# A stage woven by hand in steps of seven chunks, one norm product on ScalarE, and more convolution chunks on VectorE

## Chip, cores, metric

The kernel runs on one core of a Trainium2 chip. The metric is the device time of one execution in microseconds. A core has five engines, each with its own queue that runs in order: TensorE (PE, with its weight loads shown apart as PEld), VectorE (DVE), ScalarE (ACT), GpSimd (POOL) and SyncE (SP), which starts the DMAs. Semaphores join the queues.

## The reference, cut to what matters

Four layers run over x of shape (2, 56, 56, 128): two images, 3136 tokens each, 128 channels. The change lies in layer 1 (a selective scan over four groups of 32 channels, called heads), and in the way from it to layer 2's attention; one small reordering reaches layer 0.

```python
def _vss_block(x, p):
    return x + _ss2d(_layernorm(x, p['ln1_w'], p['ln1_b']), p)
...
# layer 1, with prev of one head going into the next
prev = _vss_block(chunks[0], p) + vss_skip * chunks[0]
outs = [prev]
for i in range(1, g):
    s = prev + chunks[i]
    prev = _vss_block(s, p) + vss_skip * s
    outs.append(prev)
x_res = cvm_skip * x_orig + jnp.concatenate(outs, axis=3)
x = _layernorm(x_res, final_ln_w, final_ln_b)
...
# inside _ss2d: project in, 3x3 depthwise convolution, silu, four scans, then
y = _layernorm(y, p['out_norm_w'], p['out_norm_b']) * jax.nn.silu(z)
return y @ p['out_proj_w'].T
...
# layer 2
t = _to_tokens(x)
t = t + _L2_attn_ref(_ln_t(t))      # queries, keys and values are all _ln_t(t)
```

## The kernel before

Tokens are tiled into 28 rows of 112 for each image; four rows make a chunk of 448 tokens, so there are seven chunks, numbered 0 to 6. X holds all tokens of both images by token (112 partitions x 28 x 2 x 128). In layer 1 both images go together: 64 inner channels of each fill the 128 partitions.

Layer 1 has four scan blocks, one a head. Between them lie short stages, run by `Layer1.run`. For head 1 to 3 its loop goes over steps c = 0 to 7: `after(head - 1, c)` finishes chunk c of the head before, `before(head, c)` prepares chunk c of the next. Ahead of head 0, layer 0's own loop calls `before` in the same manner. After the last head the loop calls `after`, `last` (the final norm) and `chunk` of attention 2 for each chunk: this is the stage between layer 1's last scan and attention 2 (the second of the four layers is layer 1, counted from zero). Steps that follow one another in a stage:

- `gated_tokens` (L486 to L507): pm, the mean over channels by a matmul (PE); yc = y - pm (VectorE, L490); its square (ScalarE, L492); yc times the gate (GpSimd, L494); then for each of four token tiles three products, pv, p1, p2 (PE, L504, "p" in the text: 24 matmul records); rs, a square root on ScalarE (L506) and its reciprocal on VectorE (L507).
- `after` (L861 to L866): t = p1 times rs, plus p2 (VectorE), plus the old token values (GpSimd, L863); s and xo, two multiply-adds into the head's own values and into X (VectorE, L864, L866).
- `layernorm_tokens` (L77 to L84): sum, mean, subtraction (VectorE), square (ScalarE), sum of squares (VectorE), root (ScalarE), reciprocal (VectorE), product (GpSimd, L84). It is used for a head's input (nrm), for the final norm (X, with statistics in stf), and for attention 2's input (U, with stu).
- `last` multiplies X by a weight and adds a bias, both on GpSimd (L876): X's three GpSimd products are L84 and twice L876.
- `Attention2.chunk`: U, the norm of X; for each image four transposes to channels (PE, L1102), an evacuation that goes in turn to VectorE and ScalarE (L64, L68), and the key tiles: transposes back (PE, L1242) and another evacuation.
- `before` (L822 to L846): the head's input, its norm, four transposes pt (PE, L830) and hT (ScalarE, L831), a projection (L833) written into pad (ScalarE, L834), a padded image; a second projection and a silu for the gate z (L845, L846). At step c it also convolves chunk c - 1, which needs one row of chunk c in pad.
- `conv_rows`: the convolution by nine PE matmuls with diagonal weights (L455), or by nine taps on VectorE (L459, L461); then silu (ScalarE, L462) and a copy in column order (GpSimd, L463). Even steps go to VectorE, odd ones to PE:

```python
"DVE" if c % 2 == 0 else "PE",
```

The order of the instructions outside the scans comes from the framework's scheduler, which may move an instruction ahead of others within its engine; inside a block marked `manual_schedule` (as the scans are) the program order stands. Pools give the buffers: `mid1` has two of each name, `pmid1` one of each PSUM name, `pa2` two PSUM banks. After the woven stage, `mixer_filters` (L1297 to L1309) builds filter tables before attention 2 begins its first scores (L1034); the mixer's small weight sums (L1345 to L1364, L1666) are scheduled into the stage by VectorE's order. The next scan begins with a spread matmul, b (L359), and a product, h (L412).

Of the kernel before, what the change touches and what calls it, by code (L numbers as in the profile page):

```python
# [21 lines left out]
B = 2  # L22
# [47 lines left out]

def layernorm_tokens(k, out, x, sq, st, d, by=None):


    nc = k.nc
    g = x.shape[1]
    mean, var = st[:, 0, :], st[:, 1, :] if by is None else by
    nc.vector.tensor_reduce(mean, x, AX.X, ALU.add)  # L77
    nc.vector.tensor_scalar_mul(mean, mean, 1.0 / d)
    nc.vector.tensor_tensor(out, x, mean.unsqueeze(2).to_broadcast([TP, g, d]), ALU.subtract)
    nc.scalar.activation(sq, out, AF.Square)  # L80
    nc.vector.tensor_reduce(var, sq, AX.X, ALU.add)
    nc.scalar.activation(var, var, AF.Sqrt, bias=k.eps[:TP], scale=1.0 / d)
    nc.vector.reciprocal(var, var)
    nc.gpsimd.tensor_tensor(out, out, var.unsqueeze(2).to_broadcast([TP, g, d]), ALU.mult)  # L84

# [389 lines left out]

def gated_tokens(k, pools, nch, y, gate, avg, mean, w1, w2, c, nb):

# [7 lines left out]
    for ci in range(nch):  # L485
        nc.tensor.matmul(pm, lhsT=avg, rhs=y[ci][:, cs], start=ci == 0, stop=ci == nch - 1)  # L486
    sq, yz = [], []
    for ci in range(nch):
        yc = sp.tile([128, CH], F32, name=f"yc{ci}")
        nc.vector.tensor_tensor(yc, y[ci][:, cs], pm, ALU.subtract)  # L490
        s = one.tile([128, CH], F32, name=f"sq{ci}")
        nc.scalar.activation(s, yc, AF.Square)  # L492
        sq.append(s)
        nc.gpsimd.tensor_tensor(yc, yc, gate[ci], ALU.mult)  # L494
        yz.append(yc)
    n = w1[0].shape[-1]
# [3 lines left out]
    for i in range(4):  # L500
        ts = slice(TP * i, TP * (i + 1))
        for out, m, rhs in ((pv[:, nb * i : nb * (i + 1)], sq, [mean] * nch), (p1[:, i], yz, w1), (p2[:, i], gate, w2)):
            for ci in range(nch):
                nc.tensor.matmul(out, lhsT=m[ci][:, ts], rhs=rhs[ci], start=ci == 0, stop=ci == nch - 1)  # L504
    rs = sp.tile([TP, 4 * nb], F32, name="rs")
    nc.scalar.activation(rs, pv, AF.Sqrt, bias=k.eps[:TP])  # L506
    nc.vector.reciprocal(rs, rs)  # L507
    return p1, p2, rs
# [45 lines left out]
def layer0(k, d, big, follow):  # L554
# [3 lines left out]
    with ExitStack() as ctx:  # L558
# [42 lines left out]
        with ExitStack() as sctx:  # L601
# [65 lines left out]
            def after(b, pools, c, outs, bias):  # L667
# [9 lines left out]
                for ci in range(2):  # L677
# [6 lines left out]
                    gate.append(z)  # L684
                p1, p2, rs = gated_tokens(k, pools, 2, y, gate, avg, avg[:, 0:1], outs[0], outs[1], c, 1)
                t = one.tile([TP, 4, C], F32, name="t")
# [40 lines left out]
class Layer1:  # L727
# [82 lines left out]
    def before(self, head, pools, c, pad):  # L810
# [27 lines left out]
        if c > 0:  # L838
            conv_rows(
                k, (sp, vp), pad, self.diag, W["taps"], W["conv_b"], self.row, self.col, c - 1,  # L840
                "DVE" if c % 2 == 0 else "PE",
            )
# [6 lines left out]

    def after(self, head, pools, c):  # L850
        k, nc, D, R = self.k, self.k.nc, self.D, self.R
        sp, pp = pools
        gate = [self.z[:, CH * c : CH * (c + 1)]]
        p1, p2, rs = gated_tokens(k, (sp, pp, sp), 1, [self.y], gate, self.avg, self.mean, *self.outs, c, B)
        t = sp.tile([TP, 4 * B, D], F32, name="t")
# [5 lines left out]
        nc.vector.tensor_tensor(t, tokens(p1), rs.unsqueeze(2).to_broadcast([TP, 4 * B, D]), ALU.mult)  # L861
        nc.vector.tensor_tensor(t, t, tokens(p2), ALU.add)
        nc.gpsimd.tensor_tensor(t, t, s, ALU.add)  # L863
        nc.vector.scalar_tensor_tensor(s, s, R["vss_skip"], t, ALU.mult, ALU.add)  # L864
        xo = self.chunk(self.channels(head), c)
        nc.vector.scalar_tensor_tensor(xo, xo, R["cvm_skip"], s, ALU.mult, ALU.add)  # L866

    def last(self, sp, c):

# [3 lines left out]
        st = sp.tile([TP, 2, 4 * B], F32, name="stf")  # L873
        layernorm_tokens(k, xv, xv, sq, st, C)
        for op, n in ((ALU.mult, "final_ln_w"), (ALU.add, "final_ln_b")):
# [17 lines left out]
    def run(self, follow):  # L893
# [3 lines left out]
        for head in range(1, 5):  # L897
            self.scans.run()
            with ExitStack() as ctx:
# [4 lines left out]
                else:  # L904
                    sp = ctx.enter_context(k.pool("mid1", 2))
                    chunk = follow(ctx)
                for c in range(NCH + 1):
                    if c < NCH:
                        self.after(head - 1, (sp, pp), c)
                    if head < 4:  # L910
                        self.before(head, (sp, pp, self.vp), c, pad)
                    elif c < NCH:
                        self.last(sp, c)
                        chunk(c)

# [160 lines left out]
class Attention2:  # L1076
# [9 lines left out]
    def start(self, ctx):  # L1086
        self.sp = ctx.enter_context(self.k.pool("a2u", 2))
        self.pp = ctx.enter_context(self.k.pool("pa2", 2, psum=True))
        return self.chunk

    def chunk(self, c):
# [5 lines left out]
        flat = "p j b c -> p (j b) c"  # L1097
        layernorm_tokens(k, U.rearrange(flat), k.X[:, 4 * c : 4 * (c + 1)].rearrange(flat), sq, st, C)
        for b in range(B):
            pt = bank(self.pp, "pt")[:, 0:CH]  # L1100
            for i in range(4):
                nc.tensor.transpose(pt[:, TP * i : TP * (i + 1)], U[:, i, b, :], k.ident[:TP, :TP])  # L1102
            k.evacuate(self.uT[b][:, CH * c : CH * (c + 1)], pt)
            key_tiles(k, bank(self.pp, "pt"), self.uT[b], self.V[b], c)

# [882 lines left out]
```

## Time and profile before

| what | value |
|---|---|
| runs of the kernel before | 9179.0 us median of 3 (9177.25 to 9184.39) |
| the profiled execution | 9196.55 us |
| its span in the trace | 9194.7 us |
| mean granted TensorE clock | 0.947 |
| GpSimd's product L425 in the scans | 3755.4 us, 2048 times, 1859 ns each |
| VectorE's scan L353 | 2788.5 and 900.7 us, 1536 and 512 times |
| convolution matmuls L455 | 468 in all, 538 ns median, 1115 at most |
| stage from the first way into head 0 | 2766 to 2904 us |
| the ways into heads 1, 2 and 3 | 3547 to 3657, 4292 to 4401, 5037 to 5152 us |
| stage from the last scan to attention 2 | 5795 to 5947 us |

A line of a timeline gives the start in us, the duration in us, the engine, the line of the kernel, the operation, and what it writes and reads by name; in square brackets how long the engine had been idle and what released it. A line of windows gives the busy time of each engine in that stretch. Busy shares of the whole span average over stages with different limits, so a stage is read from its own windows.

### The profile page before, as it was taken

The page shows a single profiled execution, that of the slowest core. Times are in us where ns is not written, and L with a number is a line of the kernel's source. Part 1 is how long each engine was busy: PE and PEld are TensorE (multiplying, and loading weights), DVE is VectorE, ACT ScalarE, POOL GpSimd, SP SyncE. Part 2 cuts the span into 40 slices and gives each one's busy share as a digit, 9 for nine tenths or more (in the row PEclk, how much of TensorE's full clock was granted, in tenths as well). Part 3 has the DMA queues.
Part 4 walks back from the last instruction along what each step waited for, and adds up shares of the span by engine and source line. Part 5 has one row for each costly group of instructions (what it writes and reads, how often), then busy time and mean ns, then how long its engine had stood idle before and what let it go on. Part 6 is the DMA issues. An engine that isn't in the chain of part 4 may idle for free.

```text
span 9194.7 us, 93730 instructions
## 1 busy us (share of the span) xinstructions
PE 8062.6 (88%) x28825; PEld 4797.1 (52%) x28825; DVE 7113.2 (77%) x7587; ACT 3845.9 (42%) x6551; POOL 6325.5 (69%) x4023
## 2 busy tenths in 40 slices
PE   7888888888888888888888888699999999999998
PEld 3444445444445444444444444355688888874555
DVE  8999998999996997998899799611466666665442
ACT  4555545555555555555554555234211111114331
POOL 5999996999995996997899699666311111115551
PEclk9999999999998998999999899699999999999998
DMA  5666664666663994986798599100233333320003
GB/s 155 222 220 220 222 214 129 220 220 220 221 220 102 229 225 120 223 227 157 190 227 208 136 228 227 49 3 3 71 104 101 109 93 106 95 62 7 14 5 129
DMA packets 781377, 1364.55 MB, mean 148 GB/s; under 512 B 133213, under 2 KB 406494, under 8 KB 780842
## 3 DMA queue, kind: packets, MB, share of 16 engines
q1 hardware_dynamic: 780874, 1358.56, 52.4%
q8 instruction: 228, 3.74, 0.2%
q14 instruction: 275, 2.25, 0.1%
HBM read 1318.63 MB, written 39.60 MB: 148 GB/s over the span
## 4 chain that ended last, share of the span: by engine, by line
PE 38%; DVE 11%; issue 5%; ACT 3%; POOL 2%; DMA 1%; SPq 0%; DVEq 0%; POOLq 0%; ACTq 0%
PE cv L1516 12%; PE av L1028 6%; PE sc L1034 5%; DVE h L353 5%; PE pj L1630 4%; DVE h L412 3%; PE acc L373 2%; DMA c<-rows 1%; ACT a L334 1%; PE b L161 1%; PE cv L1578 1%; PE pcv L455 1%; POOL p L425 1%; PE every L1796 1%; PE lo L969 1%
## 5 line engine op out<-in xcount | busy, mean ns | idle before, releaser
L425 POOL TENSOR_TENSOR p<-h,c 128x784 f32<-128x784 f32 x2048 | 3755.4, 1859 | 125.5 <-DVE h L353 38.6
L373 PE MATMUL acc<-p,ident 128*128 128x392 f32 x8192 | 2990.4, 499 | 23.0 <-POOL p L425 21.8
L353 DVE TENSOR_TENSOR_SCAN h<-a,state,h 128x784 f32<-128x784 f32 x1536 | 2788.5, 1837 | 48.7 <-ACT a L334 27.4
L373 PEld LDWEIGHTS acc<-p,ident 128*128 128x128 f32 x8192 | 1487.3, 193 | 1043.8 <-POOL p L425 80.4
L412 DVE TENSOR_TENSOR h<-du,b 128x784 f32<-128x784 f32 x1408 | 1332.7, 947 | 96.5 <-PE b L359 91.4
L334 ACT ACTIVATE a<-delta,L0A 128x784 f32<-128x784 f32 x1024 | 939.3, 918 | 968.5 <-DVE h L353 965.8
L334 ACT ACTIVATE a<-delta,L1A 128x784 f32<-128x784 f32 x1024 | 939.0, 917 | 918.9 <-DVE h L353 916.1
L359 PE MATMUL b<-three,sel 96*128 96x512 bf16 (+1 forms) x2816 | 730.9, 342 | 572.7 <-DVE h L412 475.6
L428 POOL TENSOR_TENSOR h<-du,b 128x784 f32<-128x784 f32 x640 | 1187.8, 1856 | 0.0
L1047 POOL TENSOR_TENSOR total<-total,e 128x448 f32<-128x448 f32 (+1 forms) x644 | 735.8, 1143 | 325.1 <-ACT e L1036 285.2
L359 PEld LDWEIGHTS <-sel 96*128 96x128 bf16 x2816 | 282.6, 100 | 1243.2 <-issue 1065.4
L353 DVE TENSOR_TENSOR_SCAN h<-a,h 128x784 f32<-128x784 f32 x512 | 900.7, 1777 | 33.7 <-ACT a L334 23.4
L1529 DVE TENSOR_TENSOR u<-u,cv 128x512 f32<-128x512 f32 x1024 | 623.4, 679 | 326.9 <-PE cv L1516 325.6
L1560 POOL TENSOR_TENSOR u<-u,S 128x1024 f32<-128x1024 f32 x64 | 150.1, 2367 | 1039.2 <-DVE S L1529 1039.2
L1036 ACT ACTIVATE e<-sc 128x448 f32<-128x448 f32 (+1 forms) x700 | 377.5, 543 | 722.8 <-PE sc L1034 594.8
L1531 ACT COPY u<-cv 128x512 f32<-128x512 f32 x256 | 149.4, 587 | 826.7 <-PE cv L1516 773.3
L1630 PE MATMUL pj<-u,Wm 128*128 128x196 f32 (+8 forms) x1536 | 351.5, 382 | 5.7 <-DVE A L1636 5.7
L1034 PE MATMUL sc<-big 128*128 128x448 f32 (+1 forms) x700 | 323.4, 548 | 12.3 <-ACT e L1036 12.3
L1028 PE MATMUL av<-e,big 128*128 128x448 f32 (+1 forms) x700 | 320.7, 545 | 1.2 <-DVE e L1041 1.1
L1610 POOL TENSOR_TENSOR both<-mpm 128x512 f32<-128x512 f32 x32 | 40.6, 1270 | 395.0 <-DVE Wm L1666 271.5
L1630 PEld LDWEIGHTS pj<-u,Wm 128*128 128x128 f32 x1536 | 266.6, 191 | 70.4 <-issue 45.7
L973 DVE TENSOR_REDUCE m<-lo 112x1 f32<-112x448 f32 x392 | 229.2, 617 | 95.4 <-PE lo L969 95.1
(438 smaller groups left out, 10866.9 us busy)
## 6 DMA issues: line engine op xcount, KB each, us to landing
c<-rows SPq DMA_DIRECT2D x1024, 392.0 KB, 4.0
c<-rows SPq DMA_DIRECT2D x2048, 196.0 KB, 4.8
b<-rows SPq DMA_DIRECT2D x320, 392.0 KB, 4.5
b<-rows SPq DMA_DIRECT2D x640, 196.0 KB, 4.6
H<-raw SPq DMA_DIRECT2D x32, 1568.0 KB, 7.6
wC<-win SPq DMA_DIRECT2D x64, 576.0 KB, 6.2
w<-in_L_weight_dram SPq DMA_DIRECT2D x52, 512.0 KB, 5.3
wA<-win SPq DMA_DIRECT2D x64, 384.0 KB, 5.5
```

What stands on the lines that cost most here:

```text
L334: self.k.nc.scalar.activation(x["a"], g["delta"][ci], AF.Exp, scale=self.w["A"](g["kd"], ci, x["n"]))
L353: self.k.nc.vector.tensor_tensor_scan(h, a, h, start, ALU.mult, ALU.add)
L359: self.k.nc.tensor.matmul(ps[:, c0:c1], lhsT=self.w["selB"](x["n"]), rhs=x["g"]["three"][:, c0:c1], start=True, stop=True)
L373: nc.tensor.matmul(job["acc"][:, i, 0:392], lhsT=self.k.ident, rhs=x["p"][:, 392 * i : 392 * (i + 1)], start=False, stop=n == NS - 1,)
L412: nc.vector.tensor_tensor(one["h"], one["g"]["du"][one["ci"]], one["b"], ALU.mult)
L425: nc.gpsimd.tensor_tensor(now["p"], now["h"], now["c"], ALU.mult)
L428: nc.gpsimd.tensor_tensor(three["h"], three["g"]["du"][three["ci"]], three["b"], ALU.mult)
L1028: nc.tensor.matmul(acc, lhsT=V[b][:n, j, :], rhs=e[:n], start=j == 0, stop=j == NKT - 1)
L1034: nc.tensor.matmul(ps[:n], lhsT=keys[b][:, KT * j : KT * j + n], rhs=q, start=True, stop=True)
L1047: nc.gpsimd.tensor_tensor(total[:n], total[:n], e[:n], ALU.add)
L1516: self.k.nc.tensor.matmul(ps[:, b], lhsT=v[:, C * b : C * (b + 1)], rhs=h, start=i == 0, stop=i == len(terms) - 1)
L1630: nc.tensor.matmul(ps[:, lo - c0 : hi - c0], lhsT=Ws[f][:, eo, r, :], rhs=u[:, b, f, lo - a0 : hi - a0], start=f == 0, stop=f == 1,)
```

## The change

Seven chunks of the stage after the last head run as generators, each cut into 22 steps by `yield`. `woven` starts a new chunk every five ticks and advances every active chunk by one step in each tick, the oldest first; the block is marked `manual_schedule`, so this order stands in every queue. In that stage U's last product, 112 x 1024 on GpSimd, becomes eight ScalarE copies with a scale, 112 x 128 each. The pool `pa2` gets four PSUM banks instead of two. In layer 0, which uses the same gated function, the two subtractions now come ahead of the two squares. In `before`, step 5's convolution goes to VectorE for heads 1 to 3, and steps 3 and 5 for head 0: nine matmuls less and nine taps more for each.

```diff
--- before.py
+++ after.py
@@ -68,7 +68,28 @@
             self.nc.scalar.copy(out, in_)
 
 
-def layernorm_tokens(k, out, x, sq, st, d, by=None):
+def all_of(steps):
+
+
+    while True:
+        try:
+            next(steps)
+        except StopIteration as e:
+            return e.value
+
+
+def woven(stages, apart):
+
+    stages, active, at = list(stages), [], 0
+    while stages or active:
+        if stages and at % apart == 0:
+            active.append(stages.pop(0))
+        active = [one for one in active if next(one, active) is not active]
+        at += 1
+
+
+def layernorm_steps(k, out, x, sq, st, d, by=None, last="POOL"):
+
 
 
     nc = k.nc
@@ -77,11 +98,24 @@
     nc.vector.tensor_reduce(mean, x, AX.X, ALU.add)
     nc.vector.tensor_scalar_mul(mean, mean, 1.0 / d)
     nc.vector.tensor_tensor(out, x, mean.unsqueeze(2).to_broadcast([TP, g, d]), ALU.subtract)
+    yield
     nc.scalar.activation(sq, out, AF.Square)
+    yield
     nc.vector.tensor_reduce(var, sq, AX.X, ALU.add)
+    yield
     nc.scalar.activation(var, var, AF.Sqrt, bias=k.eps[:TP], scale=1.0 / d)
+    yield
     nc.vector.reciprocal(var, var)
-    nc.gpsimd.tensor_tensor(out, out, var.unsqueeze(2).to_broadcast([TP, g, d]), ALU.mult)
+    if last == "POOL":
+        nc.gpsimd.tensor_tensor(out, out, var.unsqueeze(2).to_broadcast([TP, g, d]), ALU.mult)
+    else:
+        yield
+        for i in range(g):
+            nc.scalar.activation(out[:, i], out[:, i], AF.Copy, scale=var[:, i : i + 1])
+
+
+def layernorm_tokens(*args, **more):
+    all_of(layernorm_steps(*args, **more))
 
 
 def tokens_to_channels(k, pool, dst, src):
@@ -473,7 +507,7 @@
     nc.gpsimd.memset(pad[:, :, PAD - 1 : PAD], 0.0)
 
 
-def gated_tokens(k, pools, nch, y, gate, avg, mean, w1, w2, c, nb):
+def gated_steps(k, pools, nch, y, gate, avg, mean, w1, w2, c, nb):
 
 
 
@@ -485,14 +519,18 @@
     for ci in range(nch):
         nc.tensor.matmul(pm, lhsT=avg, rhs=y[ci][:, cs], start=ci == 0, stop=ci == nch - 1)
     sq, yz = [], []
+    yield
     for ci in range(nch):
         yc = sp.tile([128, CH], F32, name=f"yc{ci}")
         nc.vector.tensor_tensor(yc, y[ci][:, cs], pm, ALU.subtract)
+        yz.append(yc)
+    yield
+    for ci, yc in enumerate(yz):
         s = one.tile([128, CH], F32, name=f"sq{ci}")
         nc.scalar.activation(s, yc, AF.Square)
         sq.append(s)
         nc.gpsimd.tensor_tensor(yc, yc, gate[ci], ALU.mult)
-        yz.append(yc)
+    yield
     n = w1[0].shape[-1]
     pv = pp.tile([TP, 4 * nb], F32, name="pv")
     p1 = pp.tile([TP, 4, n], F32, name="p1")
@@ -502,8 +540,10 @@
         for out, m, rhs in ((pv[:, nb * i : nb * (i + 1)], sq, [mean] * nch), (p1[:, i], yz, w1), (p2[:, i], gate, w2)):
             for ci in range(nch):
                 nc.tensor.matmul(out, lhsT=m[ci][:, ts], rhs=rhs[ci], start=ci == 0, stop=ci == nch - 1)
+    yield
     rs = sp.tile([TP, 4 * nb], F32, name="rs")
     nc.scalar.activation(rs, pv, AF.Sqrt, bias=k.eps[:TP])
+    yield
     nc.vector.reciprocal(rs, rs)
     return p1, p2, rs
 
@@ -682,7 +722,7 @@
                     z = sp.tile([128, CH], F32, name=f"z{ci}")
                     nc.scalar.activation(z, ps, AF.Silu, bias=W["in_b"][:, 2 + ci : 3 + ci])
                     gate.append(z)
-                p1, p2, rs = gated_tokens(k, pools, 2, y, gate, avg, avg[:, 0:1], outs[0], outs[1], c, 1)
+                p1, p2, rs = all_of(gated_steps(k, pools, 2, y, gate, avg, avg[:, 0:1], outs[0], outs[1], c, 1))
                 t = one.tile([TP, 4, C], F32, name="t")
                 nc.vector.tensor_tensor(t, p1, rs.unsqueeze(2).to_broadcast([TP, 4, C]), ALU.mult)
                 nc.vector.tensor_tensor(xr, xr, p2, ALU.add)
@@ -838,7 +878,7 @@
         if c > 0:
             conv_rows(
                 k, (sp, vp), pad, self.diag, W["taps"], W["conv_b"], self.row, self.col, c - 1,
-                "DVE" if c % 2 == 0 else "PE",
+                "DVE" if c in ((2, 3, 4, 5, 6) if head == 0 else (2, 4, 5, 6)) else "PE",
             )
         if c < NCH:
             ps = vp.tile([128, CH], F32, name="pcv")
@@ -848,10 +888,13 @@
             self.scans.first(vp)
 
     def after(self, head, pools, c):
+        all_of(self.after_steps(head, pools, c))
+
+    def after_steps(self, head, pools, c):
         k, nc, D, R = self.k, self.k.nc, self.D, self.R
         sp, pp = pools
         gate = [self.z[:, CH * c : CH * (c + 1)]]
-        p1, p2, rs = gated_tokens(k, (sp, pp, sp), 1, [self.y], gate, self.avg, self.mean, *self.outs, c, B)
+        p1, p2, rs = yield from gated_steps(k, (sp, pp, sp), 1, [self.y], gate, self.avg, self.mean, *self.outs, c, B)
         t = sp.tile([TP, 4 * B, D], F32, name="t")
 
         def tokens(p):
@@ -860,18 +903,20 @@
         s = self.chunk(self.prev, c)
         nc.vector.tensor_tensor(t, tokens(p1), rs.unsqueeze(2).to_broadcast([TP, 4 * B, D]), ALU.mult)
         nc.vector.tensor_tensor(t, t, tokens(p2), ALU.add)
+        yield
         nc.gpsimd.tensor_tensor(t, t, s, ALU.add)
+        yield
         nc.vector.scalar_tensor_tensor(s, s, R["vss_skip"], t, ALU.mult, ALU.add)
         xo = self.chunk(self.channels(head), c)
         nc.vector.scalar_tensor_tensor(xo, xo, R["cvm_skip"], s, ALU.mult, ALU.add)
 
-    def last(self, sp, c):
+    def last_steps(self, sp, c):
 
         k, nc = self.k, self.k.nc
         xv = self.chunk(k.X, c)
         sq = sp.tile([TP, 4 * B, C], F32, name="sqf")
         st = sp.tile([TP, 2, 4 * B], F32, name="stf")
-        layernorm_tokens(k, xv, xv, sq, st, C)
+        yield from layernorm_steps(k, xv, xv, sq, st, C)
         for op, n in ((ALU.mult, "final_ln_w"), (ALU.add, "final_ln_b")):
             nc.gpsimd.tensor_tensor(xv, xv, self.R[n].unsqueeze(1).to_broadcast([TP, 4 * B, C]), op)
 
@@ -904,14 +949,23 @@
                 else:
                     sp = ctx.enter_context(k.pool("mid1", 2))
                     chunk = follow(ctx)
+                if head == 4:
+
+                    def end(c):
+                        yield from self.after_steps(3, (sp, pp), c)
+                        yield
+                        yield from self.last_steps(sp, c)
+                        yield
+                        yield
+                        yield from chunk(c)
+
+                    with k.tc.manual_schedule():
+                        woven((end(c) for c in range(NCH)), 5)
+                    continue
                 for c in range(NCH + 1):
                     if c < NCH:
                         self.after(head - 1, (sp, pp), c)
-                    if head < 4:
-                        self.before(head, (sp, pp, self.vp), c, pad)
-                    elif c < NCH:
-                        self.last(sp, c)
-                        chunk(c)
+                    self.before(head, (sp, pp, self.vp), c, pad)
 
 
 
@@ -1085,7 +1139,7 @@
 
     def start(self, ctx):
         self.sp = ctx.enter_context(self.k.pool("a2u", 2))
-        self.pp = ctx.enter_context(self.k.pool("pa2", 2, psum=True))
+        self.pp = ctx.enter_context(self.k.pool("pa2", 4, psum=True))
         return self.chunk
 
     def chunk(self, c):
@@ -1095,12 +1149,16 @@
         sq = self.sp.tile([TP, 4 * B, C], F32, name="squ")
         st = self.sp.tile([TP, 2, 4 * B], F32, name="stu")
         flat = "p j b c -> p (j b) c"
-        layernorm_tokens(k, U.rearrange(flat), k.X[:, 4 * c : 4 * (c + 1)].rearrange(flat), sq, st, C)
+        x = k.X[:, 4 * c : 4 * (c + 1)].rearrange(flat)
+        yield from layernorm_steps(k, U.rearrange(flat), x, sq, st, C, last="ACT")
+        yield
         for b in range(B):
             pt = bank(self.pp, "pt")[:, 0:CH]
             for i in range(4):
                 nc.tensor.transpose(pt[:, TP * i : TP * (i + 1)], U[:, i, b, :], k.ident[:TP, :TP])
             k.evacuate(self.uT[b][:, CH * c : CH * (c + 1)], pt)
+        yield
+        for b in range(B):
             key_tiles(k, bank(self.pp, "pt"), self.uT[b], self.V[b], c)
 
     def run(self, early, inputs):
```

## The prediction, made before the change was run

> **What bounds the kernel now.** I read the page first: the busy shares, then the chain of work that ended last.
>
> ```profile
> PE 8062.6 (88%) x28825; PEld 4797.1 (52%) x28825; DVE 7113.2 (77%) x7587; ACT 3845.9 (42%) x6551; POOL 6325.5 (69%) x4023
> ...
> PE 38%; DVE 11%; issue 5%; ACT 3%; POOL 2%; DMA 1%; SPq 0%; DVEq 0%; POOLq 0%; ACTq 0%
> ```
>
> These are averages over stages. The change touches five short ones, so I asked for the busy times of these windows: the way into the first head, the three between heads, and the stage from layer 2 to attention 2, which I call the woven stage, with its tail.
>
> ```profile
> 2766.00:2904.00 138.00, 123.44 (x535) 78.66 (x534) 68.19 (x137) 76.99 (x115) 38.40 (x41) 0.89 0.12 29
> 3547.00:3657.00 110.00, 96.14 (x331) 55.53 (x329) 52.51 (x114) 58.51 (x88) 31.87 (x37) 0.77 0.12 28
> 4292.00:4401.00 109.00, 95.38 (x339) 54.13 (x338) 56.22 (x116) 58.60 (x88) 36.99 (x39) 0.81 0.13 30
> 5037.00:5152.00 115.00, 99.93 (x340) 57.10 (x338) 56.14 (x117) 58.70 (x89) 36.63 (x39) 0.78 0.12 29
> 5795.00:5930.00 135.00, 66.47 (x284) 51.85 (x282) 99.55 (x149) 35.57 (x62) 78.37 (x45) 0.56 0.00 0
> 5930.00:5947.00 17.00, 4.36 (x8) 1.84 (x8) 8.74 (x26) 2.21 (x5) 1.21 (x2) 0.52 0.32 70
> ```
>
> After the window's length come PE, PEld, DVE, ACT and POOL busy, then TensorE's granted clock. The first four windows (472 us) lean on PE, the fifth on VectorE (99.55) and GpSimd (78.37), and none of the engines is full. So these stages are chains of waits, and the order of each queue decides. The fifth, in GpSimd's timeline (start, duration):
>
> ```profile
> 5876.29 1.90 POOL L84 TENSOR_TENSOR X<-X,stf 112x1024 f32<-112x1024 f32 x1 [5.27 <-DVE stf L83]
> ...
> 5897.64 2.60 POOL L84 TENSOR_TENSOR X<-X,stf 112x1024 f32<-112x1024 f32 x1
> 5900.32 2.68 POOL L876 TENSOR_TENSOR X<-X,L1final_ln_w 112x1024 f32<-112x1024 f32 x1
> 5903.08 3.21 POOL L876 TENSOR_TENSOR X<-X,L1final_ln_b 112x1024 f32<-112x1024 f32 x1
> 5910.59 1.90 POOL L84 TENSOR_TENSOR X<-X,stf 112x1024 f32<-112x1024 f32 x1 [4.30 <-DVE stf L83]
> ```
>
> The final norm's product on X starts at 5816.86 for chunk 0 and 5910.59 for chunk 6: 93.7 us over six intervals, 15.6 each. The last U transpose starts at 5928.53 and ends 5929.48, 18.9 after that product. Then 17 us of filter set-up follow (memset, two DMAs, 21 sums), the same in both kernels.
>
> The way from head 0 to head 1, in PE's timeline:
>
> ```profile
> 3639.53 1.67 PE L455 MATMUL pcv<-pad,diag 128*128 128x448 f32 x4
> 3641.12 1.02 PE L845 MATMUL pcv<-big,L1in_w 64*128 64x448 f32 x2
> 3642.07 0.57 PE L830 MATMUL pt<-ident,nrm 112*64 112x112 f32 x4
> 3643.28 1.02 PE L833 MATMUL pcv<-big,L1in_w 64*128 64x448 f32 x2 [0.63 <-ACT big L831]
> 3644.13 0.91 PE L845 MATMUL pcv<-big,L1in_w 64*128 64x448 f32 x2
> 3646.06 8.62 PE L455 MATMUL pcv<-pad,diag 128*128 128x448 f32 x18 [1.02 <-ACT pad L834]
> 3654.52 0.50 PE L359 MATMUL b<-three,sel 96*128 96x512 bf16 x2
> ```
>
> The last convolution (step 7) waits for chunk 6's rows in pad, and the scan's first spread waits for it alone. What moves pad of chunk 6 moves the head.
>
> **What the Trainium skill says.** SBUF — State Buffer, "SBUF: two separate sides": VectorE and GpSimd share a pair of ports as an exclusive lock, and a two-input VectorE operation and a GpSimd one block each other whole. The trace agrees: X's product at 5816.86 took 2.77 instead of 1.90, and L866 on VectorE, begun 5817.78, took 2.12 instead of 0.48, ending as the product ended. TensorE: Matmul & The Clock Gate, "What's actually happening": the array runs at half clock until it was busy for some 3.4 us. The trace: 0.56 granted in the woven stage; the 24 matmuls of L504 take about 4.4 us there (1.1 for each of four groups) against 2.4 in the busier window of head 1 (3623.07 to 3625.5). ScalarE: Activation LUTs, "What ACT_TABLE_LOAD costs", says that an ACTIVATE with one pointer operand takes 280 ns + 0.833 ns an element, and that successive ones overlap by 93 ns; for the 128 elements of the new copies an estimate of 0.29 us each. The trace's own squares (0.42 for 256 elements, 1.06 for 1024) give 0.31.
>
> **The woven stage.** Removed from GpSimd: seven U products of 1.9 us. Added to ScalarE: 56 copies, 8 x 0.30 = 2.4 us a chunk; ScalarE is busy 35.6 of 135 us, so it has room; behind the copies on its queue stands the square of X of b, which waits for its subtraction anyway, so I cost their delay to others at nothing (2.4 us a round if that cover goes). A GpSimd chunk falls from 10.3 us (yc 1.13, t 0.72, X 1.90 + 2 x 2.34, U 1.90) to 8.4. A VectorE chunk stays near 11.5. The two further pa2 banks take away waits for a bank; I cost them at nothing. On SP's queue only one DMA changes places with its neighbour; the load of the mixer's weights still lands (5794) ahead of the stage.
>
> What decides is the fixed order: 22 steps a chunk, a new chunk every five ticks, oldest first. The instruction orders of both kernels show what this ties together. With chunk a two ahead of c, GpSimd runs X's three products of a, then yc of c; PE then runs p of c, and only behind it the U transposes of the oldest chunk z; VectorE evacuates those before it may sum the squares of X of b (one behind a); then come rs and t of c, the evacuation of z's keys, U's sum of squares, yc of the next chunk, and last the reciprocal of b, which releases the next three products. That is a ring. Its members: reciprocal and start 0.28; X's products 1.90 + 2 x 2.34 and gaps, 6.69 with starts; 1.8 to 2.9 for yc and what VectorE's two-input operations hold from GpSimd; p cold 4.1; transposes 1.0; evacuation 0.55; sum of squares 1.15; rs, t, t 0.95; keys' evacuation with its wait 0.5 to 1; U's sum of squares 1.15; yc 0.55; handovers the rest. Total T = 20.2 cold, 17.3 if p runs warm. Before, the same operations stood in an order that never tied yc, p and the U transposes of different chunks into one ring, and took 15.6.
>
> First reciprocal of X at 5815.5 (5816.58 before; the mixer's small sums now all stand ahead of it, and moving them costs what it saves). Then 16.5 (no z yet), three times 20.2, 19.1, and 14.5 (no c left): 110.7. From chunk 6's reciprocal to its last transpose 17 (X 6.7, U's reduces, square and root 5.5, eight copies 2.4, transposes, evacuation and second transposes 2.4). End 5943.2 against 5929.5, +13.7. With p warm it would be -0.6. I take +12, since some groups will run warm, and keep -1 to +17. Even is T = 17.
>
> **Heads 1 to 3.** Removed: nine matmuls of step 5, 8.5 us of PE a head (7.0 where warm). Added: nine VectorE taps, 0.45 + 8 x 0.68, pitch 0.6. They fall inside chunk 6's chain on VectorE: three before t (L862), then one between each of its operations. Before, t of chunk 6 starts at 3629.27 and the norm's reciprocal at 3637.93, and pt at 3642.07 waits for step 5's convolution. After: t 3632.1; GpSimd's sum behind a column copy, 3634.0; the chain with six taps to L79, 3639.3; the new chunk's silu now ahead of the square on ScalarE, with its table load (1.28 in the trace), so square 3641, root 3643.2, reciprocal 3643.6; product 3644.5, pt 3645.1, hT, projection and pad 3648.6. The last convolution begins 3649 instead of 3646.06: +3. PE's freed 8.5 us lie idle while it waits. Three heads: +9, between 0 (silu late enough) and +12.
>
> **Head 0.** Eighteen matmuls go (7.03 and 9.56 us), 18 taps come. Here VectorE stands idle 4.79, 6.35 and 8.30 us around the convolutions, and the chain runs through PE: step 5 takes 2883.00 to 2892.49, and chunk 6's pt and pad wait behind it until 2896.3. Walking the new order I get pad of chunk 4 at 2861 (2869 before), of chunk 5 at 2870.5 (2883), of chunk 6 at 2884 to 2886 (2896): the last convolution some 11 earlier, 1 given back as it runs colder. Layer 0's own yc pair now stands ahead of its squares; the same work, costed at nothing. -10, between -14 and 0.
>
> **Sum.** +12 + 9 - 10 = +11, on the profiled 9196.55 us (span 9194.7). The median of the runs is 9179.0, 17.5 below that execution; +11 on it is 9190.
>
> **Rivals.** Forecast: the ring costs what head 0 gains, the total stays within 0.2% (18.4 us, about what a measurement of this kernel can tell from no change): 9190, own range 9164 to 9197. Chance 0.43.
>
> Slower: the ring turns still slower, at X's products. Before, L876 once took 3.21 instead of 2.34, L84 2.77, t 1.71 instead of 0.72. In the weave VectorE's s, xo and both subtractions fall beside these products in every round; if each round pays 2 us more in four full rounds and 1 in the two partial ones, that is +10: +21, 9200; with head 0 at nothing besides, +31, 9210. It decides from +7.4 on the ring, 1.9 us a full round. For it: the exclusions are in the trace. Against: with U's product gone GpSimd holds the pair less. Chance 0.33, at 9203.
>
> Faster, by the weave: PE warm and the ring not closed, VectorE bound at 7 x 11.8 = 83 us after a fill of 19 and a tail of 17: 5797 + 119 = 5916, -13; with -10 and +6, -17; with heads even, -23, 9156. Against: GpSimd's order puts yc behind X's products. Chance 0.12.
>
> Faster, by convolutions: PE's freed time reaches the end of each head. Its windows are PE-heavy (96 of 110); 3 x -6, head 0 -14 and a warm weave -0.6 make -33, 9146. Against: pad of chunk 6. Chance 0.12.
>
> That the weave doesn't reach the queues is excluded by the instruction order.
>
> The range goes from 9152 to 9212, from most of the fast cases to the slow one with head 0 at nothing. Faster 0.24, same 0.43, slower 0.33.
>
> **What would show it.** Right: X's products 19 to 21 us apart with yc just behind them, U's last transpose near 5943 less what the heads shifted; step 7's convolution about 3 us later after each of heads 0 to 2, and 10 us earlier ahead of head 0. Wrong: products at most 16 us apart; pt of chunk 6 starting earlier than before; step 7's start ahead of head 0 unmoved.

## The result, and the profile after

| what | before | changed |
|---|---|---|
| median of the runs, us | 9177.99 (14 runs, 9169.89 to 9199.65) | 9202.4 (14 runs, 9185.12 to 9220.07) |
| ratio, with its 95% interval | | 1.0025 (1.0016 to 1.0034) |
| profiled execution, us | 9196.55 | 9205.31 |

The change makes the kernel slower by about 24 us. The two profiled executions differ by 8.8 us only: single runs scatter by some 10 us, and in the two traces the scans themselves drift against each other by some 10 us without any instruction of theirs having changed. So the sum is taken from the stages below, not from the two spans.

The page after, first line of the busy shares and of the chain of waits:

```profile
PE 8034.7 (87%) x28735; PEld 4777.0 (52%) x28735; DVE 7144.1 (78%) x7632; ACT 3866.0 (42%) x6608; POOL 6314.3 (69%) x4016
...
PE 45%; DVE 27%; issue 13%; ACT 8%; POOL 4%; DMA 2%; SPq 1%; DVEq 0%; POOLq 0%; ACTq 0%
```

VectorE has 45 instructions more and ScalarE 57, for 45 taps and 56 copies. The chain's shares add up to 60% of the span before and to all of it here, so they can't be compared. Neither line shows where 24 us went. The windows of the five stages do (length, then PE, PEld, DVE, ACT and POOL busy, TensorE's granted clock, the DMA engines' share and GB/s):

```profile
2764.00:2898.00 134.00, 111.51 (x498) 73.29 (x497) 77.23 (x152) 82.58 (x119) 39.02 (x39) 0.82 0.12 29
3542.00:3647.00 105.00, 83.42 (x294) 48.70 (x295) 57.50 (x122) 57.40 (x87) 29.41 (x30) 0.72 0.12 29
4290.00:4391.00 101.00, 77.64 (x295) 43.56 (x295) 57.10 (x122) 57.35 (x87) 29.29 (x30) 0.78 0.13 30
5039.00:5145.00 106.00, 84.83 (x295) 49.90 (x295) 57.17 (x121) 57.57 (x87) 28.83 (x30) 0.71 0.12 29
5794.00:5940.00 146.00, 68.53 (x290) 53.45 (x289) 101.17 (x148) 51.98 (x117) 65.99 (x38) 0.58 0.00 0
```

In the woven stage GpSimd is relieved by 12 us (78.37 to 65.99), ScalarE takes 16 on, VectorE's work is unchanged at about 100, and yet the stage is longer: from its first pm matmul to the first score behind the filter set-up it takes 157.3 us instead of 146.5. Work was moved off a busy engine and time was lost, so it went into waits. Of the six intervals between X's first products of successive chunks, the second to the fifth are the full rounds, in which chunks are under way at every point of the stage. The chain of waits in one of them (start, duration, what):

```profile
5830.43 2.04 POOL X L110
...
5835.02 3.41 POOL X L921
5838.43 1.10 POOL yc L532
...
5839.57 1.01 PE p L542 x4
...
5843.94 1.49 PE pt L1158 x8
5845.43 1.52 PE pm L520 x2
5846.95 0.65 PE pt L1300 x3
5847.63 0.56 DVE big L64
5848.19 1.13 DVE stu L104
5849.32 0.53 DVE yc L525
5849.84 0.12 DVE stf L108
...
5850.03 2.04 POOL X L110
```

This is a closed ring: X's three products, yc's product behind them in GpSimd's queue, p, the U transposes and key transposes behind p in PE's, the keys' evacuation, U's sum of squares, yc and X's reciprocal on VectorE, and again X's product, 19.6 us later. GpSimd's timeline shows the same and where the long product comes from:

```profile
5850.03 2.02 POOL L110 TENSOR_TENSOR X<-X,stf 112x1024 f32<-112x1024 f32 x1 [1.73 <-DVE stf L108]
5852.14 2.41 POOL L921 TENSOR_TENSOR X<-X,L1final_ln_w 112x1024 f32<-112x1024 f32 x1
5854.63 3.41 POOL L921 TENSOR_TENSOR X<-X,L1final_ln_b 112x1024 f32<-112x1024 f32 x1
5858.00 1.13 POOL L532 TENSOR_TENSOR yc<-yc,pair 128x448 f32<-128x448 f32 x1
```

The bias addition takes 3.41 us instead of 2.34 in every full round: VectorE's subtraction for the next chunk's X runs from 5854.61 for 1.23 us and holds it off, as the exclusive lock on the ports that VectorE and GpSimd share, in SBUF — State Buffer (the Trainium skill, "SBUF: two separate sides"), has it.

The end of the way into head 1, in PE's timeline:

```profile
3632.14 0.96 PE L870 MATMUL pt<-ident,nrm 112*64 112x112 f32 x4 [10.74 <-POOL nrm L110]
3633.71 1.86 PE L873 MATMUL pcv<-big,L1in_w 64*128 64x448 f32 x2 [0.61 <-ACT big L871]
3635.36 1.70 PE L885 MATMUL pcv<-big,L1in_w 64*128 64x448 f32 x2
3636.99 8.43 PE L489 MATMUL pcv<-pad,diag 128*128 128x448 f32 x18
3646.14 0.49 PE L393 MATMUL b<-three,sel 96*128 96x512 bf16 x2 [0.72 <-ACT big L496]
```

PE stands idle for 10.74 us where step 5's convolution was: it waits for chunk 6's norm. Then the matmuls run cold, that is at half of the clock (1.70 us for L885, 0.91 for the same matmuls before), and the scan's first spread now waits 0.72 us for the silu of the last convolution, which it did not before.

To read these stages without the scans' drift I count from chunk 1's rows written into pad (the second L834, L874 after) to the next scan's first accumulator taken out (ScalarE's copy of the scan's first finished sum out of PSUM). Counted so, kernels with the same order in a stage agree within 1 to 3.5 us over fourteen traces, but for two in which chunk 2 comes late on the way into head 0 (of these below). A way into a head with other steps than these two sets is in neither column:

| stage | steps of before | steps of the change |
|---|---|---|
| way into head 0 | 149.5, 149.6 | 145.2 to 146.3, mean 146.0 of 7 |
| ways into heads 1 to 3 | 120.5 to 122.4, mean 121.2 of 15 | 124.9 to 128.4, mean 126.6 of 21 |

The sum: head 0 -3.5, heads 1 to 3 three times +5.4 = +16.1, the woven stage +10.8: +23.4 us, against 24.4 of the medians. Three of the 15 and nine of the 21 are of a slower form, in which chunk 2 comes 14 us behind chunk 1 instead of 12.5; within one form the loss is 4.5 or 5.8 us a head, so some 0.3 of the 5.4 lies in this mixture.

### The profile page after: what moved, and what is told of

Its sections match the earlier page's. It is cut to its first block, busy times and chain, and to the rows that moved or that the text cites. A ratio compares the mean times of both kernels' runs of the same rounds, so it can differ in the third digit from the quotient of the medians.

```text
span 9203.5 us, 93628 instructions
## 1 busy us (share of the span) xinstructions
PE 8034.7 (87%) x28735; PEld 4777.0 (52%) x28735; DVE 7144.1 (78%) x7632; ACT 3866.0 (42%) x6608; POOL 6314.3 (69%) x4016
## 4 chain that ended last, share of the span: by engine, by line
PE 45%; DVE 27%; issue 13%; ACT 8%; POOL 4%; DMA 2%; SPq 1%; DVEq 0%; POOLq 0%; ACTq 0%
DVE h L387 13%; PE cv L1574 12%; DVE h L446 8%; PE av L1082 5%; PE sc L1088 5%; PE acc L407 4%; PE pj L1688 4%; ACT a L368 3%; PE b L195 3%; DMA c<-rows 2%; PE b L393 1%; POOL p L459 1%; POOL h L462 1%; PE acc L421 1%; PE cv L1636 1%
## 5 line engine op out<-in xcount | busy, mean ns | idle before, releaser
L1027 DVE TENSOR_REDUCE m<-lo 112x1 f32<-112x448 f32 x392 | 229.4, 618 | 95.1 <-PE lo L1023 94.8
```

## The experiments

**The two halves alone.** First, the kernel before with the new steps only:

```diff
-                "DVE" if c % 2 == 0 else "PE",
+                "DVE" if c in ((2, 3, 4, 5, 6) if head == 0 else (2, 4, 5, 6)) else "PE",
```

> The kernel before with the new convolution steps alone. My theory: the stage between the last scan and attention 2, counted from its first pm matmul to the first score after the filter set-up, stays at 146.5 us (146.5 before, 157.3 with the whole change). The last convolution ahead of the scans comes 2.5 to 4 us later on the ways into heads 1 to 3 and 3 to 6 us earlier on the way into head 0; the sum is +4 to +8 us, ratio 1.0005 to 1.0009. Rival, that the convolutions carry most of the loss: ratio 1.0015 or more. Rival, that they gain and the weave alone loses: ratio under 1.

Measured: ratio 1.0017 (1.0007 to 1.0026). X's first product to the first score took 126.7 us, 126.6 in the kernel before (the piece ahead of it came out 2.8 longer, with the same order). The ways into heads 1 to 3 took 125.0, 125.2 and 125.0, the one into head 0 146.1: +8.1 in all in this trace, +12.6 by the means of the table above, which rest on more traces, and +16 by the medians of the runs. That is more than I expected, and the ratio is that of the first rival. The convolutions carry about half of the loss; the interval of the ratio is too wide to say more.

Second, the changed kernel with the steps of before:

```diff
-                "DVE" if c in ((2, 3, 4, 5, 6) if head == 0 else (2, 4, 5, 6)) else "PE",
+                "DVE" if c % 2 == 0 else "PE",
```

> The changed kernel with the convolution steps of before. My theory: X's first products stand 19 to 20 us apart in the four full rounds, the stage takes 157 us against 146.5, and the total is +10 to +12 us, ratio 1.0012 (1.0011 to 1.0013). Rival, that the convolutions carry most of the loss: ratio under 1.0008 with a stage that is no longer.

Measured: ratio 1.0016 (1.0007 to 1.0024). X's products stand 19.4, 20.0, 19.6 and 19.0 apart in the full rounds, the stage takes 158.0, and the ways into the heads are those of before (149.6; 120.7 to 122.4). The weave costs what its stage shows.

**One member of the ring taken away.**

```diff
-        for op, n in ((ALU.mult, "final_ln_w"), (ALU.add, "final_ln_b")):
+        for op, n in ((ALU.mult, "final_ln_w"),):
```

> The changed kernel without the addition of the final norm's bias to X (left out; the second of the two L921 operations, 3.41 us in the full rounds). Ring theory: it is a member of the ring, so X's first products come nearer by about 3.2 us in each full round, 16.2 to 16.6 apart instead of 19 to 20, and the stage shortens by 15 to 20 us. Rival, that VectorE or a cold PE sets the pace: they move by less than 1 us a round and the stage by less than 6.

Measured: 16.1, 16.5, 15.9 and 15.5 apart, 3.5 less in each round; stage 136.7, 20.6 less. An operation of 3.4 us on GpSimd, which is busy under half of the stage, comes off the time in full in every round.

**U's product back on GpSimd.**

```diff
-        yield from layernorm_steps(k, U.rearrange(flat), x, sq, st, C, last="ACT")
+        yield from layernorm_steps(k, U.rearrange(flat), x, sq, st, C)
```

> The changed kernel with U's product on GpSimd again, in the same woven order. Ring theory: it stands behind yc's product in GpSimd's queue and off the ring, so X's first products stay 19 to 20 us apart (at most 1 us more through the pair of ports), and the stage stays within 4 us of 157; in the tail the eight ScalarE copies and GpSimd's product cost nearly the same. Rival, that the product's place on GpSimd matters in itself: 21 us or more apart, stage 10 us or more longer.

Measured: 22.0 apart, stage 173.4. My number was wrong, and what the rival gave came about, but not by its mechanism. Without the copies the step generator has one `yield` less, so the U transposes move up one tick. VectorE's timeline of this kernel:

```profile
5882.61 1.23 DVE L100 TENSOR_TENSOR X<-X,stf 112x1024 f32<-112x1024 f32 x1
5892.32 0.62 DVE L64 COPY big<-pt 128x448 f32<-128x448 f32 x1 [8.49 <-PE pt L1158]
5892.86 1.21 DVE L98 TENSOR_REDUCE stu<-X 112x8 f32<-112x1024 f32 x1
```

The evacuation now stands ahead of U's sum. VectorE waits 8.49 us for the transposes and does the sum and the subtraction, some 2.5 us, afterwards; in the changed kernel it does them inside that wait. It fits the 2.4 us a round. The chain of waits of this trace goes through these operations and not through GpSimd's product of U: that ends at 5866.87 in the round before, while PE is at p until 5869.44 and only then comes to the U transposes. What the product alone would cost on GpSimd, with the order kept, was not run.

**More room between X and U, oldest first.**

```diff
                         yield from self.last_steps(sp, c)
                         yield
                         yield
+                        yield
+                        yield
                         yield from chunk(c)
```

> The weave with two more empty ticks between X's products and U's norm, still the oldest chunk first. Ring theory: yc of chunk c still stands behind X's products of chunk c - 2 on GpSimd and p behind yc, but the U transposes and U's sums no longer stand between p and the next reciprocal; worked out as 0.3 + 6.7 + 1.1 + 4.1 + 0.4 + 1.0 and some 4 of VectorE, the ring takes 17 to 18 us, and the stage 146 to 151. Rival, cold PE or VectorE as the bound: no change from 19 to 20.

Measured: 17.0 in the middle rounds, stage 149.2, as worked out. The ring is shorter and still closed through yc. Its members are not quite those I named: the chain of waits of this trace still has U's sum and subtraction (2.6 us) on VectorE between p and the reciprocal, while the bias addition takes 2.34 us instead of 3.41. The size was right in part by luck.

**Newest first, with and without that room.** The edit of `woven`, alone in the one kernel, with the two ticks in the other:

```diff
-        active = [one for one in active if next(one, active) is not active]
+        active = [one for one in active[::-1] if next(one, active) is not active][::-1]
```

> The changed kernel with the newest chunk first alone, without the two empty ticks. Ring theory: yc is free of X's products, but U's sums now stand between X's products and the next reciprocal on VectorE: 0.3 + 6.7 + 2.6 + 1.0 + 1.15 + 0.6 + 0.55 + 1.15 + 0.5 + 1.0 and handovers, 15.5 to 17 us between X's first products, stage 136 to 146 us. Rival, that newest first alone opens the ring: 12 to 13.5 us.

> The same two empty ticks, and within a tick the newest chunk first instead of the oldest. yc's product then stands ahead of X's products of the chunk two before, so p no longer waits for them. Ring theory: the ring is open, and the pace falls to VectorE's own work, 12 to 13.5 us between X's first products; the stage takes 120 to 130 us, and the kernel beats both (9150 to 9165 on the median of before). Rival, cold PE or the shared ports as the bound: 16 us or more apart, stage 140 or more.

Measured: alone 16.4 to 17.7 apart in the full rounds and a stage of 150.7, over what I had worked out. The ring through U's sums is longer than my sum of it: its chain of waits goes on through the key transposes (1.98), an evacuation and a square on ScalarE (0.59 and 0.49) and yc's product (1.14) before it comes back to X's products. With both edits 12.5, 12.7, 13.8 and 12.0 apart, and a stage of 124.8 us: 32.5 less than the change, with the same instructions on the same engines, and 21.7 less than before. GpSimd's timeline of the kernel with both:

```profile
5845.94 1.64 POOL L532 TENSOR_TENSOR yc<-yc,pair 128x448 f32<-128x448 f32 x1 [1.38 <-ACT sq L530]
5848.58 1.90 POOL L110 TENSOR_TENSOR X<-X,stf 112x1024 f32<-112x1024 f32 x1 [0.99 <-DVE stf L108]
5850.55 3.42 POOL L921 TENSOR_TENSOR X<-X,L1final_ln_w 112x1024 f32<-112x1024 f32 x1
5854.05 2.35 POOL L921 TENSOR_TENSOR X<-X,L1final_ln_b 112x1024 f32<-112x1024 f32 x1
5856.36 0.72 POOL L907 TENSOR_TENSOR t<-t,pair 112x256 f32<-112x256 f32 x1
```

yc stands ahead of X's products, and p no longer waits for them. PE is as cold as with the change (0.58 granted in this stage in both), and GpSimd is still held off by VectorE (3.42), so neither of these by itself set the old pace. VectorE, though, is held less: it is busy for 88.6 us of this stage, with the change for 101.2. Nor is the pace now VectorE's own work alone, as I had expected. In the middle rounds the chain of waits goes through another ring, 13.6 and 13.8 us long:

```profile
5842.76 0.30 ACT stf L106
5843.06 2.34 ACT U L114 x8
5845.40 0.47 ACT sq L530
...
5845.94 1.65 POOL yc L532
...
5847.64 1.01 PE p L542 x4
...
5852.01 1.29 PE pt L1302 x6
...
5855.12 1.14 DVE stf L104
...
5856.35 0.30 ACT stf L106
```

The cold p and the eight copies of U on ScalarE are members of it; what either costs here was not tried. The single run of this kernel, 9179.55 us beside 9176.98 of the one before, can't tell 9150 from 9180; the timed versions below can. I had not counted the heads' loss in what I expected of its total.

**Newest first with other convolution steps.** Steps on VectorE, everything else as in the kernel with both edits:

```diff
-                "DVE" if c in ((2, 3, 4, 5, 6) if head == 0 else (2, 4, 5, 6)) else "PE",
+                "DVE" if c in ((2, 3, 4, 5, 6) if head == 0 else (2, 4, 6)) else "PE",
```

> Newest chunk first with the two empty ticks, head 0's steps 2 to 6 on VectorE as in the change, heads 1 to 3 with steps 2, 4 and 6 as before. My theory: the stage stays near 125 us (-22 against before), the way into head 0 from the last accumulator taken out to the next one is some 4 us shorter, and heads 1 to 3 stay as before: -26 us, ratio 0.9972 (0.996 to 0.998), faster than both kernels. Rival, that the stage's gain is given back later: ratio over 0.999.

Measured: 9156.0 us beside 9187.86, ratio 0.9967 (0.9954 to 0.9979). Stage 124.8; heads 1 to 3 121.0 each. The way into head 0 gave nothing in its profiled run: chunk 2's rows came 5.3 us late (19.4 us behind chunk 1's, 14.1 in most traces). The order up to there is that of other kernels which don't show it; the last section tells what delayed them.

```diff
-                "DVE" if c in ((2, 3, 4, 5, 6) if head == 0 else (2, 4, 5, 6)) else "PE",
+                "DVE" if c in ((2, 3, 4, 6) if head == 0 else (2, 3, 4, 6)) else "PE",
```

> Newest first with the two empty ticks; step 3 instead of step 5 goes to VectorE, for all heads (steps 2, 3, 4, 6). My theory: the loss on the ways into heads 1 to 3 comes from step 5's taps inside chunk 6's chain; step 3's taps lie ahead of it, so from the last accumulator taken out to the first spread it takes 98 to 102 us (before 98 to 104, mean 101; with the change 100 to 108, mean 105). Rival, that a fourth chunk on VectorE costs wherever it stands: 104 or more in all three. On the way into head 0 step 3 alone gains at most 2 of the 4 us (135 to 137; before 137, with the change 133).

```diff
-                "DVE" if c in ((2, 3, 4, 5, 6) if head == 0 else (2, 4, 5, 6)) else "PE",
+                "DVE" if c in ((2, 4, 5, 6) if head == 0 else (2, 4, 6, 7)) else "PE",
```

> Newest first with the two empty ticks; heads 1 to 3 have steps 2, 4, 6 and 7 on VectorE, so that the last convolution isn't on PE, and head 0 has steps 2, 4, 5 and 6. Taps of step 7 take 0.45 + 8 x 0.6 = 5.3 us behind the last three of step 6 (2.1), against 8.5 cold on PE: from the last accumulator taken out to the next one 155 to 157 us in heads 1 to 3 (before 154 to 159.5, mean 156.7; with the change mean 161.5), the gain 0 to 2. Rival, VectorE's first products of the scan pushed back more than PE gains: 160 or more. On the way into head 0, step 5 alone brings the 4 us: 132 to 134 to the first spread (before 137).

Measured in the terms of the expectations: 99.8, 101.1 and 99.7 us to the first spread with step 3 in heads 1 to 3, and 156.8, 155.5 and 159.5 to the next accumulator with step 7. Counted more sharply, from chunk 1's rows to the first spread of the next scan, with steps 2, 3, 4, 6: heads 1 to 3 66.8, 66.7, 66.7 (65.5 before, mean of 15; 70.3 with the change, mean of 21), so step 3 costs 1.2 and not 4.7. Of both, 0.7 is no matter of VectorE's taps. Where the last convolution is on PE, the first spread waits 0.72 us for its silu in every way with three convolutions on PE, and not at all in those with two or four. The convolutions and projections take two PSUM buffers in turn, so an odd number puts the last convolution into the other buffer; that the spread needs just this one was not shown. Head 0: 87.5 (93.6 before, 90.2 to 90.5 with the change in six of its seven traces): my expectation there, that step 3 alone gives nearly nothing, was wrong. Step 7 on VectorE brings the first spread some 6.5 us forward (58.8 to 60.1), and the first accumulator comes out at 121.1, 121.1 and 122.4, no sooner than before: the gain is given back behind the spread. Head 0 with step 5 alone took 101.2, with chunk 2 again 5.6 us late. Both head 0 results ran against my account of it, so I repeated them:

```diff
-                "DVE" if c in ((2, 3, 4, 5, 6) if head == 0 else (2, 4, 5, 6)) else "PE",
+                "DVE" if c in ((2, 3, 4, 6) if head == 0 else (2, 4, 6)) else "PE",
```

> Newest first with the two empty ticks; head 0 has steps 2, 3, 4 and 6 on VectorE, heads 1 to 3 have 2, 4 and 6 as before. On the way into head 0, from chunk 1's rows in pad to the first spread: 87 to 89 us again (93.6 in the two runs with the steps of before, 90 with the change), since step 3 gives and step 5 doesn't. Stage 125 us, heads 1 to 3 as before. In all -22 - 6 = -28 us, ratio 0.9970 (0.996 to 0.998). Rival, that the 87.5 us of the one run with step 3 alone was chance: 91 to 94, total -22.

```diff
-                "DVE" if c in ((2, 3, 4, 5, 6) if head == 0 else (2, 4, 5, 6)) else "PE",
+                "DVE" if c in ((2, 4, 5, 6) if head == 0 else (2, 4, 6)) else "PE",
```

> As the version just above, but on the way into head 0 step 5 instead of step 3 (steps 2, 4, 5, 6). From chunk 1's rows in pad to the first spread, 94 to 97 us if there is no late chunk 2 (101 with chunk 2's rows 5.6 us late, as in the one run so far): no gain against 93.6. Rival, the step of my prediction, that step 5's matmuls hold chunk 6's rows and their release brings the gain: 86 to 90.

Measured: step 3 alone 88.7, step 5 alone 95.1. The first of the two is also the best version: 9148.27 us beside 9179.8 of the kernel before in the same series, ratio 0.9969 (0.9957 to 0.9981). It can't be told apart from the version with 0.9967; both beat the kernel before and the change. By its stages the best version gains 21.4 us in the woven one and 3.7 on the way into head 0, some 25 in all; the medians differ by 31.5, and the interval of the ratio reaches from 17 to 39 us.

The way into head 0 from chunk 1's rows:

| steps on VectorE | to the first spread, us | to the first accumulator, us |
|---|---|---|
| 2, 4, 6 | 93.6, 93.7 | 149.5, 149.6 |
| 2, 3, 4, 5, 6 | 90.2 to 90.5, once 89.5; 97.0 with chunk 2 late | 145.2 to 146.3; 152.9 |
| 2, 3, 4, 6 | 87.5, 88.7 | 144.6, 145.8 |
| 2, 4, 5, 6 | 95.1; 101.2 with chunk 2 late | 152.3; 156.6 |

Counted to the accumulator, step 3 alone is hardly better than steps 3 and 5 together: part of its lead at the spread is given back behind it.

## Why the prediction came out as it did

The measured time, 9202.4 us, lies in the range, and the forecast case does not hold: 1.0025 is beyond 0.2%, where I had put 0.43 on staying within. The time is that of the slower rival (9203), but not through it.

- **The woven stage: right, by mechanism and size.** The ring was read from the order of the queues: T = 20.2 cold forecast, 19.0 to 20.0 measured; first reciprocal of X at 5815.5 forecast, the product behind it at 5814.67 measured; six intervals 110.7 forecast, 107.9 measured; tail 17 forecast, 17.0 measured (5922.53 to 5939.56). The stage's term was +12, measured +10.8. The experiments that shorten the ring, open it and lengthen it moved the pace clearly, by 2 to 7 us a round, and mostly as worked out, so the ring is shown. The slower rival, the ring turning slower still through exclusions, did not happen: these are in it (3.41), and they were inside my sum. A detail was misread: in the example of the lock, L866 ended at 5819.90, 0.27 us behind the product on X, not with it.
- **ScalarE's copies: right.** Eight took 2.45 us at 5891.84, 0.31 each; the estimate from ScalarE: Activation LUTs (the Trainium skill, "What ACT_TABLE_LOAD costs"), 0.29, and the one from the squares, 0.31, both hold.
- **Heads 1 to 3: right in mechanism, mis-sized.** The term "Three heads: +9" measured +16.1. In head 1 chunk 6's rows came 59.5 us behind chunk 1's; in traces of before 56.2 at the same phase of chunk 2 (12.5 us), so the walk's +3 is there. What I left out stands behind pad, +2 us a head: the second projection, ahead of the last convolution as before but now cold, so that the convolution waits for it 0.5 us beyond pad; the silu that the first spread waits for (0.72); and a start of the scan that is slower in some traces (from the first spread to the accumulator 55.5 us in head 1 of the changed kernel, 57.2 in heads 2 and 3, 55.7 before; why was not shown). That step 5's taps inside chunk 6's chain are the main cause is shown by step 3's, which cost 1.2.
- **Head 0: this step failed.** "Here VectorE stands idle" was right and the conclusion wrong: the term -10 measured -3.5. The walk has 8 of its 10 to 12 us at chunk 4 already, ahead of step 5, so these are step 3's; its words, though, have chunk 6 wait behind step 5, whose matmuls take 9.56 us. Alone, step 5 loses 1.5 us to the first spread and step 3 gains 5 to 6 (to the accumulator 2.7 lost and 3.7 to 4.9 gained). So step 5 brought nothing, and step 3 less than the walk had. Chunk 3's rows came 5.6 us later against chunk 1's in the changed kernel (37.7 instead of 32.1), which my walk did not have: taps of step 3 now stand between its norm's operations on VectorE, and pt of chunk 3 behind layer 0's p matmuls on PE (norm's product 2837.54, pt 2841.30). With step 5 alone they come at 32.5. Chunk 4's rows then gained 3.6 of the 8 forecast, chunk 6's 6 of 10 to 12, and the colder end took 2.5 back, not 1.

  What step 3 gives can be read in PE's timeline of the kernel before: its convolution stands ahead of the matmuls that finish layer 0's chunk 4.

```profile
2841.66 7.03 PE L455 MATMUL pcv<-pad,diag 128*128 128x448 f32 x18
2848.63 1.02 PE L845 MATMUL pcv<-big,L1in_w 64*128 64x448 f32 x2
2849.57 0.55 PE L504 MATMUL pv<-avg,sq 128*112 128x1 f32 x4
```

  With step 3 alone on VectorE chunk 4's rows come 3.3 and 5.0 us earlier than before, with step 5 alone 2.0 later. Why chunk 6 gains more than this with step 3 was not traced further.
- **The rival by convolutions**, PE's freed time reaching the end of each head, fell: PE stood idle for it, 10.74 us in head 1.

So the sum of +11 was short by 12 us: 7 in heads 1 to 3 and 6.5 in head 0, less 1 in the stage.

## What to carry to other kernels

When stages of several tiles are woven by hand, write down for each engine's queue what now stands behind what, and follow the queues round: if the walk comes back to its start within one round, the sum of its members is the pace, however idle each engine is. A long operation on a slow engine wants the next tile's short one ahead of it and its own consumer late; here two such edits of order took the same instructions from 19.6 to 12.7 us a round. Then look for the next ring; here it went through the copies that had been moved to ScalarE. Before work is moved to an idle engine, find whose chain it will stand inside: the same nine taps cost 4.7 us as step 5 and 1.2 as step 3.

## What was not expected of the hardware

How far a collision of one microsecond can reach. PE's timeline on the way into head 0, first of the version with the ratio 0.9967, then of the kernel with both edits and the steps of the change; up to here both have the same order:

```profile
2815.94 0.64 PE L870 MATMUL pt<-ident,nrm 112*64 112x112 f32 x4 [2.19 <-POOL nrm L110]
2816.38 1.73 PE L719 MATMUL pz<-hout,L0in_w 128*128 128x448 f32 x2
2821.62 1.84 PE L520 MATMUL pm<-pair,avg 128*128 128x448 f32 x2
2823.39 1.86 PE L873 MATMUL pcv<-big,L1in_w 64*128 64x448 f32 x2
```

```profile
2815.64 0.57 PE L870 MATMUL pt<-ident,nrm 112*64 112x112 f32 x4 [1.11 <-POOL nrm L110]
2816.05 0.93 PE L719 MATMUL pz<-hout,L0in_w 128*128 128x448 f32 x2
2818.76 1.00 PE L520 MATMUL pm<-pair,avg 128*128 128x448 f32 x2
2819.69 1.02 PE L873 MATMUL pcv<-big,L1in_w 64*128 64x448 f32 x2
```

In the first, VectorE's subtraction ahead of it (L100) took 1.50 us instead of 0.41: a GpSimd addition (L715), released by a DMA, began 0.04 us before it, in the second 0.01 us after it. So PE waited 2.19 instead of 1.11, and from there each matmul takes nearly twice as long: 1.73 instead of 0.93, 1.84 instead of 1.00, with a granted clock of 0.50 from 2818 on instead of 1.00. One microsecond became 5.3 by chunk 2's rows. The other trace with chunk 2 late shows the same pair (1.52; 2.21). The collision does not always have this end: with newest first alone the subtraction took 1.49 and PE waited 2.18, the clock stayed at 1.00, and chunk 2 came only 1.1 us late. The half clock after idling is what TensorE: Matmul & The Clock Gate (the Trainium skill, "What's actually happening") describes, but it gives some 3.4 us of idle for it; here a recorded wait of 2.2 us was enough twice, and once it was not. Whether such flips also make whole runs scatter by 10 to 20 us was not tried.

Against that, a stage repeats closely where the clock doesn't flip: ways into heads with the same order gave 64.8 to 65.4 us from chunk 1's rows to the first spread in trace after trace, with a second value near 66.6. A change of 4 us that a series of runs can't resolve is plain in one trace, counted inside the stage.
